# One unit's keys through DRAM, the last projection by rows, and a new order for an attention and feed-forward kernel

## The chip, the cores and the metric

The kernel runs on one core of a Trainium2 chip. The core has a matmul engine (TensorE, called PE in the profile; its weight loads are shown as PEld), a vector engine (DVE), a scalar engine (ACT), GpSimd (POOL, hardly used here) and SyncE (SP), whose queue issues all the transfers between on-chip memory (SBUF) and DRAM. Matmuls write to PSUM, eight banks of 128 x 512 f32. The engines run side by side and wait for each other by semaphores. The metric is device time in microseconds (us), the median of several executions; smaller is better.

## What is computed

The inputs are x (8 batches of 112 rows of 512) and a context (8 batches of 375 rows of 256). First comes cross attention with 16 heads of 128, then a feed-forward layer whose matmuls work on values rounded to 8-bit integers:

```
def attention(h, ctx):
    q = rmsnorm((h @ Wq).reshape(B, Sq, H, D), gq)
    k = rmsnorm((ctx @ Wk).reshape(B, Skv, H, D), gk)
    v = (ctx @ Wv).reshape(B, Skv, H, D)
    attn = softmax(einsum('bqhd,bkhd->bhqk', q, k) / sqrt(D))
    return einsum('bhqk,bkhd->bqhd', attn, v).reshape(B, Sq, H * D) @ Wo

def ffn(x):                                   # Q = 127
    a, sa = quantize_rowwise(x)               # round(x * Q / max|row|), max|row|
    w1, s1 = quantize_global(W1)
    h = gelu((a @ w1.T) * (sa * s1 / Q**2) + B1)
    b, sb = quantize_rowwise(h)
    w2, s2 = quantize_global(W2)
    return (b @ w2.T) * (sb * s2 / Q**2) + B2

x = x + attention(layernorm(x), ctx)
x = x + ffn(layernorm(x))
```

Inside the feed-forward layer, a row's layer norm multiplies the whole row by one positive number, the reciprocal root of its variance. Rounding by the row's largest magnitude divides that number out again, so the rounded row needs only x minus its mean; the root is wanted later, in the factor that scales the product back.

## The kernel before

The batches are taken in four pairs, and the 16 heads in four groups of four. A pair with a group is numbered G (16 of them, `NGG`), one batch with one group is a unit u (32). For each unit the kernel makes keys (three tiles of 128 context rows, 512 wide), norms and transposes them, makes scores against the transposed queries, a softmax, and weighs the context rows with the probabilities (`weigh`). Per G it then multiplies by the value weights (`values`) and by the output weights (`project`), whose result is added up, transposed, in the tile aT of the pair. After a pair's fourth group the sum is turned back to rows, added to x (`residual` or `sum_add`), and the feed-forward layer begins. The 112 rows of batch 0 are dealt out to the 16 spare rows of the other seven batches, so there are seven feed-forward batches. In the last pair, batches 6 and 7 are the tail: their hidden values are handled in four pieces of 512 columns to keep all engines going.

Nearly every transpose goes through DRAM: DVE transposes blocks of 32 x 32, four sends write the blocks to DRAM in their new places, and one fetch reads the whole back. Early work that cannot wait for this is transposed on PE by a matmul with the identity: the tokens of the first pair (`token_turn`), the first queries (`query_turn`), the first unit's keys (`key_turn`), the context rows of the first two batches (`rows_turn`) and the last unit's probabilities (`prob_turn`).

The order of all work is written out. Each step has a short name, and four scripts (one for each pair, given to `play`) list name.index words; the index counts from the script's pair, so that R.-6 in the fourth script is index 0. Within PE, DVE, ACT and SP the instructions run exactly in this order (`in_written_order`). An instruction that waits holds up all behind it on its engine, and a transfer that waits holds up all later transfers on SP. PSUM has two rings of four banks, one for scores and one for everything else (`mm_tile`); a new tile waits until the tile four before it on its ring has been read out. The names that matter here:

- kh, k0 to k2: key matmuls; kc copies them out of PSUM (ACT), kq squares (ACT), kr sums (DVE); ka, kb, ke, kd make the reciprocal root by Ln and Exp on ACT and a refinement on DVE; kn scales (DVE); kt makes blocks (DVE); ks sends, kf fetches (SP). kv and kw are the way through PE.
- xs, xa to xd, xm, xt, xk, xy: statistics, root, norm, turning and keeping of the tokens; index 7 is the last batch, whose rows are dealt out to the spare rows of the other batches' tokens.
- ct, ck: context rows through PE and their copies; cb, cs, cf, co: by blocks, send, fetch, ordering copy (ACT).
- Q, S, qt, qs, qf, G: queries, their sums of squares (ACT), blocks (DVE), send, fetch, gain; qv, qw, qx: the way through PE.
- s0 to s3 scores, x0 and x1 their maxima (DVE), e the exponentials (ACT), iv the reciprocal, n the scaling (ACT), z blocks (DVE), ps and pf send and fetch, pt and pk the way through PE; w weighing (PE) and v its copy (ACT).
- o, u, p, a: values, their copy, projection, addition for a whole pair; O, U, P, A the same for one batch, used for the last group alone.
- ra turns the sum back (PE), rb adds it to x (DVE); st statistics, fa to fd root, fi norm and maximum, fq rounding, ti and tj the turn of the rounded rows, h hidden matmuls, i their scaling and bias, g gelu (ACT), mx maxima, es scale, qp and qq rounding, tp and tk the turn, Y or y the output matmuls, yo the last addition, yd the send.
- jl, jm, ja, js, jr: loading the feed-forward weights in 1 MB pieces, their maxima (2.28 us each on DVE), scaling and rounding; lq, lk, lv, lo, lx, ly, lc, lf, l7: loads.

Before the first keys, PE runs `WARM` matmuls on zeros (L116).

Of the kernel before, what the change touches and what calls it, by code (L numbers as in the profile page):

```python
# [9 lines left out]
F32 = mybir.dt.float32  # L10
# [20 lines left out]
def xattn_ffn_kernel(  # L31
# [16 lines left out]
    nc = tc.nc  # L48
# [21 lines left out]
    WARM = 3  # L70
# [397 lines left out]
    def rows_turn(b, j0, j1):  # L468
        pt = T["pc", b] = mm_tile(f"pc_{b}_{j0}")
        for j in range(j0, j1):  # L470
            for k in range(KCC):
                nc.tensor.transpose(
                    pt[:, (j - j0) * CC + k * P : (j - j0) * CC + (k + 1) * P],
                    T["cT", b][:, k, j * P : (j + 1) * P], ident,
                )

    def rows_keep(b, j0, j1):
        if j0 == 0:
            T["c", b] = work.tile([P, NJ, CC], F32, tag="c", name=f"c_{b}", bufs=3)
        nc.scalar.copy(  # L480
            T["c", b][:, j0:j1, :].rearrange("p j c -> p (j c)"), T.pop(("pc", b))[:, : (j1 - j0) * CC]
        )

# [33 lines left out]
    for n, (j0, j1) in enumerate(((0, 2), (2, 3))):  # L517
        step(f"ct{n}", BP, rows_turn, j0, j1)
        step(f"ck{n}", BP, rows_keep, j0, j1)
        step(f"cb{n}", BP, rows_blocks, n)  # L520
        step(f"co{n}", BP, rows_order, n)
# [331 lines left out]
    def weigh(u, k):  # L853
        b = batch_of(u)
        after(*[((f"co{n}" if b >= BP else f"ck{n}"), b) for n in range(2)])
# [46 lines left out]
    def project(G, lo, n, c0):  # L902
        if n == TP:
            after(("u0", G), ("u1", G))
        else:
            after((f"U{lo // S}", G))
# [20 lines left out]

    for n in range(2):
# [6 lines left out]
        step(f"P{n}", NG, project, n * S, S, 0)  # L935
        step(f"A{n}", NG, project_add, n * S, S, 0)
# [19 lines left out]
    def turn_sum(b):  # L956

        p, i = divmod(b, BP)
        if p == NPAIR - 1:
            after((f"A{i}", NGG - 1))  # L960
        else:
            after(("a0", p * NG + NG - 1), ("a1", p * NG + NG - 1))
        pa = T["pa", b] = mm_tile(f"pa_{b}")
        for c in range(KC):
            nc.tensor.transpose(pa[:S, c * P : (c + 1) * P], T["aT", p][:, c, i * S : (i + 1) * S], ident)
# [47 lines left out]
    def stats(b):  # L1013
        after(("rb" if b >= B - BP else "rn", b), ("zf", b))
# [4 lines left out]
    def row_absmax(src, name):  # L1019
        m = small.tile([P, 1], F32, tag="rowmax", name=name)  # L1020
# [8 lines left out]
    def norm_in(b):  # L1029
        after(("fd", b))  # L1030
        xn = T["xn2", b] = ffn.tile([P, C], F32, tag="y", name=f"xn2_{b}")
        nc.vector.tensor_scalar(xn, x2_of(b), T["mv2", b][:, 0:1], T["rstd2", b], ALU.subtract, ALU.mult)
        T["m1", b] = row_absmax(xn, f"m1_{b}")
        T["d1", b] = dequant_scale(T["m1", b], absw1, f"d1_{b}")
# [6 lines left out]
    def quantize_in(b):  # L1041
        quantize_rows(home("xq", b, [P, C], BF16), T["xn2", b], quant_scale(T["m1", b], P))
# [41 lines left out]
    def hidden_keep(b, n):  # L1084
        after(("lb", 0))
# [27 lines left out]
    def pieces_scale(b):  # L1113
        after(*[(f"mx{n}", b) for n in range(NF4)])
        m = small.tile([P, 1], F32, tag="rowmax", name=f"m2_{b}")
# [71 lines left out]
    step("fi", BP, norm_in)  # L1187
    step("fq", BP, quantize_in)
# [18 lines left out]
    for n in range(2):  # L1207
# [7 lines left out]
        cz.0 lk.0 cz.1 lf.0 lf.1 lx.0 l7.0 gl.0 lc.1 kh.0 jl.0 lk.1 lq.0 jl.3 jl.6 kh.1 xs.1 xs.0 xa.1  # L1215
        xc.1 xs.7 ct0.0 kc0.0 xa.0 xb.7 k0.1 kc1.0 xb.1 xd.1 xc.0 xm.1 xa.7 kq0.0 xc.7 k1.1 kr0.0 kq1.0
        kc2.0 xb.0 xd.0 kc0.1 kr1.0 ck0.0 ct0.1 xm.0 kq2.0 xt.1 xd.7 kc1.1 cz.2 xt.0 kr2.0 ck0.1 k2.1
        kb.0 ka.0 xm.7 ke.0 kq0.1 kd.0 xk.0 kn2.0 xt.7 xk.1 gm.0 kn0.0 kv2.0 xk.7 jm.0 kc2.1 xl.0 kv0.0
        kq1.1 lq.1 k0.2 kw0.0 kw2.0 kn1.0 xy.0 xy.1 kr0.1 kv1.0 kr1.1 kq2.1 Q0.0 kr2.1 kb.1 ka.1 jm.3
        kc0.2 ke.1 Q1.0 qt0.0 kw1.0 qs0.0 lx.1 kd.1 jl.1 kn1.1 qv0.0 kn0.1 S0.0 kt0.1 k1.2 kq0.2 kn2.1  # L1220
# [181 lines left out]
```

## Time and profile before

| | |
|---|---|
| median of 3 runs | 719.77 us (719.55 to 721.48) |
| profiled execution | 720.28 us |
| its span | 718.5 us, so 1.78 us lie around it |
| PE busy | 702.7 us, 98% |
| DVE busy | 537.3 us, 75% |
| ACT busy | 433.6 us, 60% |
| DMA engines, mean busy share | 85% for the one queue in use |
| last matmul ends | 714.3 us |

The profile comes from one execution. Times in it count from the start of its span. "Idle before" is the time that an engine stood just ahead of an instruction, with the engine, tile and line that let it go on. A 512-column matmul of f32 is two passes in the trace, and passes overlap: the mean duration of one (593 ns for the keys) is longer than the time from one start to the next (0.43 us), which is what a pass costs when PE is full. A PE that is shown busy therefore means that passes lie close, and costs on PE are best taken from start to start.

### The profile page before, as it was taken

Reading aid. Unit: us, or ns where it says so; the run is one execution under the profiler, and the core shown is the slowest. Engines: PE = TensorE matmul, PEld = TensorE weight load, DVE = VectorE, ACT = ScalarE, POOL = GpSimd, SP = SyncE. Lnnn points to the kernel's source line nnn. Section 1 sums busy time; section 2 is a strip of 40 time slices with the busy share of each in tenths; the row PEclk is TensorE's granted clock in tenths of the full one; section 3 lists DMA queues with packets and bytes.
Section 4 is the critical chain, followed back from the end, with each engine's and each line's share of the span. In section 5 each row is a group of like instructions: output and inputs, shape, how many; then the busy total and the mean of one; then the engine's idle time right before and its main releaser. Section 6 shows DMA issues by size and latency. Waiting matters only on the chain.

```text
span 718.5 us, 8555 instructions
## 1 busy us (share of the span) xinstructions
PE 702.7 (98%) x2398; PEld 413.3 (58%) x2410; DVE 537.3 (75%) x1234; ACT 433.6 (60%) x1129; POOL 2.4 (0%) x10
## 2 busy tenths in 40 slices
PE   9999999999999999999999999999999999999976
PEld 4444456655657564745656465564657455667742
DVE  6997888887876677747857787868774898964395
ACT  5677576636475756556466556666755566627325
POOL 0000000000000000000000000000000000000000
PEclk9999999999999999999999999999999999999999
DMA  8799999989988999999898989999999889998201
GB/s 304 266 280 298 294 298 282 301 268 290 282 308 244 293 285 313 269 275 310 227 289 286 295 265 287 287 240 305 292 257 291 237 256 272 259 290 282 34 1 44
DMA packets 131246, 187.85 MB, mean 261 GB/s; under 512 B 34864, under 2 KB 90800, under 8 KB 130560
## 3 DMA queue, kind: packets, MB, share of 16 engines
q1 hardware_dynamic: 131200, 187.32, 85.1%
q8 instruction: 19, 0.31, 0.2%
q14 instruction: 27, 0.22, 0.1%
HBM read 124.55 MB, written 59.45 MB: 256 GB/s over the span
## 4 chain that ended last, share of the span: by engine, by line
PE 85%; DVE 5%; ACT 4%; DMA 3%; SPq 1%; issue 1%; POOL 0%; ACTq 0%; DVEq 0%; POOLq 0%
PE pkk L650 19%; PE pu L860 17%; PE pw L910 13%; PE pq L532 12%; PE sc L758 10%; PE po L887 6%; PE py L1159 2%; PE ph L1080 2%; DMA pT<-pd 1%; PE pkk L660 1%; DMA kT<-kd 1%; ACT probs L780 1%; DMA qr<-q 1%; DMA qss<-s 1%; ACT qsq L547 1%
## 5 line engine op out<-in xcount | busy, mean ns | idle before, releaser
L650 PE MATMUL pkk<-wk,cT 128*128 128x512 f32 x372 | 171.8, 593 | 0.3 <-DVE hid L1089 0.3
L860 PE MATMUL pu<-pT,c 128*128 128x448 f32 (+1 forms) x384 | 152.3, 540 | 1.0 <-DMA pT<-pd 1.0
L860 PEld LDWEIGHTS pu<-pT,c 128*128 128x128 f32 (+1 forms) x384 | 72.5, 190 | 71.3 <-issue 61.7
L780 ACT ACTIVATE probs<-sc,bias,rq 112x375 f32<-112x375 f32 x128 | 84.1, 663 | 47.8 <-DVE bias L773 47.8
L650 PEld LDWEIGHTS pkk<-wk,cT 128*128 128x128 f32 x372 | 70.0, 190 | 72.3 <-issue 60.9
L910 PEld LDWEIGHTS pw<-oT,wo 128*128 128x128 f32 x544 | 98.2, 190 | 9.8 <-issue 6.5
L910 PE MATMUL pw<-oT,wo 128*128 128x224 f32 (+1 forms) x544 | 101.8, 343 | 0.6 <-ACT oT L897 0.6
L532 PE MATMUL pq<-wq,xnT 128*128 128x512 f32 x224 | 100.2, 592 | 0.0
L758 PE MATMUL sc<-kT,qT 128*112 128x384 f32 x256 | 92.4, 486 | 0.3 <-DMA kT<-kd 0.2
L670 ACT COPY kk<-pkk 128x512 f32<-128x512 f32 x96 | 55.2, 580 | 58.6 <-DVE kz L698 25.6
L797 DVE STREAM_TRANSPOSE pz<-probs 128x384 f32<-128x384 f32 x120 | 63.7, 558 | 21.1 <-ACT probs L791 18.2
L791 ACT ACTIVATE probs<-probs,inv 112x375 f32<-112x375 f32 x128 | 72.1, 605 | 8.9 <-DVE inv L788 8.9
L771 DVE TENSOR_REDUCE top<-sc 112x1 f32<-112x375 f32 x128 | 63.8, 535 | 18.0 <-PE sc L758 17.5
L681 DVE TENSOR_REDUCE kss<-ksq 128x4 f32<-128x512 f32 x96 | 63.1, 668 | 14.0 <-ACT ksq L675 14.0
L532 PEld LDWEIGHTS pq<-wq,xnT 128*128 128x128 f32 x224 | 42.4, 190 | 49.6 <-issue 46.5
L758 PEld LDWEIGHTS sc<-kT,qT 128*112 128x112 f32 x256 | 44.7, 177 | 38.9 <-issue 16.7
L675 ACT ACTIVATE ksq<-kk 128x512 f32<-128x512 f32 x96 | 59.5, 628 | 6.4 <-DVE kss L681 6.0
L688 DVE TENSOR_TENSOR kk<-kk,rk 128x512 f32<-128x512 f32 x96 | 62.9, 675 | 0.5
L698 DVE STREAM_TRANSPOSE kz<-kk 128x512 f32<-128x512 f32 x93 | 62.3, 690 | 0.9 <-issue 0.4
L871 ACT COPY wc<-pu 128x448 f32<-128x448 f32 x64 | 33.5, 531 | 36.6 <-PE pu L860 36.6
L887 PEld LDWEIGHTS po<-wc,wv 128*128 128x128 f32 x272 | 49.1, 190 | 8.0 <-issue 4.1
L887 PE MATMUL po<-wc,wv 128*128 128x224 f32 (+1 forms) x272 | 53.1, 344 | 0.0
(122 smaller groups left out, 590.8 us busy)
## 6 DMA issues: line engine op xcount, KB each, us to landing
kd<-kz SPq DMA_DIRECT2D x124, 192.0 KB, 4.0
kT<-kd SPq DMA_DIRECT2D x31, 768.0 KB, 6.4
pT<-pd SPq DMA_DIRECT2D x30, 672.0 KB, 6.1
pd<-pz SPq DMA_DIRECT2D x90, 192.0 KB, 4.4
wq<-in_wq SPq DMA_DIRECT2D x16, 1024.0 KB, 7.7
wo<-in_wo SPq DMA_DIRECT2D x16, 1024.0 KB, 7.8
wv<-in_wv SPq DMA_DIRECT2D x16, 512.0 KB, 5.8
wk<-in_wk SPq DMA_DIRECT2D x15, 512.0 KB, 6.2
```

The lines of the kernel that those rows point to most:

```text
L532: nc.tensor.matmul(pq[:, :GW], T["xnT", p][:, k, i * P : (i + 1) * P], T["wq", G][:, k, :], start=(k == 0), stop=(k == KC - 1),)
L650: nc.tensor.matmul(pk[:, :GW], T["cT", batch_of(u)][:, k, j * P : (j + 1) * P], T["wk", u // BP][:, k, :], start=(k == 0), stop=(k == KCC ...
L681: nc.vector.tensor_reduce(T["kss", u][:, j, :], T.pop(("ksq", u, j)).rearrange("p (h d) -> p h d", d=D), AX.X, ALU.add)
L688: nc.vector.tensor_tensor(kv, kv, T["rk", u][:, j, :].unsqueeze(2).to_broadcast([P, HG, D]), ALU.mult)
L758: nc.tensor.matmul(sc[:S, :SKP].rearrange("p (j i r) -> p j i r", j=NJ, r=BK), T["qT", G, i][:, h, :], T["kT", u][:, :, :, h, :].rearrange ...
L771: nc.vector.tensor_reduce(top[:, h : h + 1], T["sc", u, h0 + h][:S, :SK], AX.X, ALU.max, negate=True)
L780: nc.scalar.activation(p_bufs[h][:S, :SK], T["sc", u, h][:S, :SK], AF.Exp, bias=T["bias", u, h0][:, h - h0 : h - h0 + 1], scale=rq_of(u, h ...
L791: nc.scalar.mul(p_bufs[h][:S, :SK], p_bufs[h][:S, :SK], T["inv", u][:, h : h + 1])
L797: nc.vector.transpose(T["pz", u][:, :, :, :, h, :].rearrange("p a f j q -> p j a f q"), p_bufs[h].rearrange("p (j a r) -> p j a r", j=NJ, ...
L860: nc.tensor.matmul(pu[:, : HG * S], T["c", b][: ROWS[j], j, k * P : (k + 1) * P], T["pT", u][: ROWS[j], :, j, :, :].rearrange("p f h q -> ...
L887: nc.tensor.matmul(po[:, (h - h0) * n : (h - h0 + 1) * n], T["wv", G][:, k, h * D : (h + 1) * D], T["wc", G][:, k, h, :, :].rearrange("p b ...
L910: nc.tensor.matmul(pw[:, (c - c0) * n : (c - c0 + 1) * n], T["wo", G][:, h, c * P : (c + 1) * P], T["oT", G][:, h, lo : lo + n], start=(h ...
```

## The change

1. `WARM` goes from 3 to 2.
2. `rows_turn` and `rows_keep` are gone: the context rows of batches 0 and 1 go by blocks and DRAM like those of the other six (cb, cs, cf, co).
3. The keys of unit 0 go by blocks and DRAM (kt, ks, kf); kv and kw are no longer called.
4. The last group's projection is made per batch with the transposed values as the stationary operand and the output weights as the moving one (`project_rows`, R). Its result stands in rows and is added to x directly (`rows_add`, rc). The sum of the first three groups is turned back and added before that (ra, rb).
5. The feed-forward norm (fi) only subtracts the mean, and no longer waits for the root; the root is multiplied into the row maximum in a new step (fe), which the hidden values' scaling (i) waits for.
6. All four scripts are ordered anew.

```
-    WARM = 3
+    WARM = 2
...
-    for n, (j0, j1) in enumerate(((0, 2), (2, 3))):
-        step(f"ct{n}", BP, rows_turn, j0, j1)
-        step(f"ck{n}", BP, rows_keep, j0, j1)
+    for n in range(2):
         step(f"cb{n}", BP, rows_blocks, n)
...
+    def project_rows(i):
+
+        after((f"U{i}", NGG - 1))
+        pr = T["pr", i] = mm_tile(f"pr_{i}")
+        for h in range(HG):
+            nc.tensor.matmul(
+                pr[:S, :], T["oT", NGG - 1][:, h, i * S : (i + 1) * S], T["wo", NGG - 1][:, h, :],
+                start=(h == 0), stop=(h == HG - 1),
+            )
+
+    def rows_add(i):
+        x2 = T["x2", NPAIR - 1][:S, i, :]
+        after(("rb", B - BP + i))
+        nc.vector.tensor_tensor(x2, x2, T.pop(("pr", i))[:S, :], ALU.add)
+
+    step("R", BP, project_rows)
+    step("rc", BP, rows_add)
...
-        step(f"P{n}", NG, project, n * S, S, 0)
-        step(f"A{n}", NG, project_add, n * S, S, 0)
...
     def turn_sum(b):
...
-        if p == NPAIR - 1:
-            after((f"A{i}", NGG - 1))
-        else:
-            after(("a0", p * NG + NG - 1), ("a1", p * NG + NG - 1))
+        after(("a0", NGG - 2), ("a1", NGG - 2))
...
     def norm_in(b):
-        after(("fd", b))
+
+
+        after(("st", b))
         xn = T["xn2", b] = ffn.tile([P, C], F32, tag="y", name=f"xn2_{b}")
-        nc.vector.tensor_scalar(xn, x2_of(b), T["mv2", b][:, 0:1], T["rstd2", b], ALU.subtract, ALU.mult)
+        nc.vector.tensor_scalar(xn, x2_of(b), T["mv2", b][:, 0:1], None, ALU.subtract)
         T["m1", b] = row_absmax(xn, f"m1_{b}")
-        T["d1", b] = dequant_scale(T["m1", b], absw1, f"d1_{b}")
+
+    def scale_in(b):
+        after(("fi", b), ("fd", b))
+        m = small.tile([P, 1], F32, tag="rowmax2", name=f"m1r_{b}")
+        nc.vector.tensor_tensor(m, T["m1", b], T["rstd2", b], ALU.mult)
+        T["d1", b] = dequant_scale(m, absw1, f"d1_{b}")
...
     def hidden_keep(b, n):
-        after(("lb", 0))
+        after(("lb", 0), ("fe", b))
```

The start of the first script and the end of the last, before and after:

```
-        cz.0 lk.0 cz.1 lf.0 lf.1 lx.0 l7.0 gl.0 lc.1 kh.0 jl.0 lk.1 lq.0 jl.3 jl.6 kh.1 xs.1 xs.0 xa.1
-        xc.1 xs.7 ct0.0 kc0.0 xa.0 xb.7 k0.1 kc1.0 xb.1 xd.1 xc.0 xm.1 xa.7 kq0.0 xc.7 k1.1 kr0.0 kq1.0
-        kc2.0 xb.0 xd.0 kc0.1 kr1.0 ck0.0 ct0.1 xm.0 kq2.0 xt.1 xd.7 kc1.1 cz.2 xt.0 kr2.0 ck0.1 k2.1
...
+        cz.0 lk.0 l7.0 cz.1 cz.2 lf.0 lf.1 lx.0 lc.1 xs.7 lv.0 gl.0 xb.7 kh.0 cb0.0 lk.1 lq.0 jl.0 jl.3
+        kh.1 xs.1 xs.0 xa.1 xa.7 xc.1 xb.0 xa.0 xb.1 xc.0 k0.1 xc.7 xd.0 kc0.0 xd.7 kq0.0 xm.7 kc1.0
+        kr0.0 k1.1 kc2.0 xd.1 kq2.0 xm.0 kq1.0 xm.1 kc0.1 kr1.0 xt.1 kc1.1 xt.7 kr2.0 xt.0 kb.0 ka.0
+        cb1.0 ke.0 k0.2 xk.7 kd.0 xk.0 xl.0 kn2.0 kq0.1 cs.0 kn1.0 xk.1 xy.1 kn0.0 k2.1 xy.0 kq1.1 kt0.0
+        kt2.0 Q0.0 kc2.1 kt1.0 kr0.1 ks.0 kr1.1 kq2.1 gm.0 kr2.1 kb.1 lx.1 k1.2 jm.3 qv0.0 kc0.2 ka.1
+        qw0.0 ke.1 cf.0 kd.1 Q1.0 qx0.0 qt0.0 kc1.2 kn2.1 qs0.0 S0.0 kn0.1 kf.0 kt0.1 lq.1 kn1.1 kt1.1
+        k0.3 S1.0 kt2.1 sa.0 qv1.0 sb.0 ks.1 xs.3 k1.3 kc0.3 xb.3 jm.0 kc1.3 kq0.3 s1.0 co0.0 qt1.0 k2.3
...
-        v0.6 qh0.-1 pt2.7 v1.6 pt1.7 qh1.-1 pk2.7 O0.3 pk1.7 te.-1 w0.7 U0.3 P0.3 v0.7 w1.7 A0.3 ra.0
-        v1.7 O1.3 rb.0 st.0 fb.0 U1.3 fa.0 P1.3 fc.0 fd.0 fi.0 fq.0 A1.3 ti.0 bo.0 ra.1 tj.0 rb.1 h0.0
-        st.1 h1.0 i0.0 fa.1 fc.1 h2.0 i1.0 g0.0 fb.1 h3.0 i2.0 fd.1 g2.0 fi.1 fq.1 i3.0 ti.1 y0.-1 tj.1
...
+        pt2.7 v0.6 w1.6 te.-1 ra.1 v1.6 pk2.7 O0.3 rb.1 n1.7 pt1.7 U0.3 ra.0 pk1.7 R.-6 rb.0 w0.7 rc.-6
+        st.0 fi.0 w1.7 v0.7 fq.0 fa.0 fc.0 ti.0 v1.7 tj.0 fb.0 h0.0 fd.0 fe.0 h1.0 i0.0 bo.0 g0.0 h2.0
+        i1.0 O1.3 i2.0 mx0.0 g2.0 h3.0 mx2.0 U1.3 g1.0 R.-5 i3.0 mx1.0 g3.0 mx3.0 es.0 qp1.0 qp0.0 y0.-1
+        rc.-5 qq0.0 st.1 fi.1 fa.1 y1.-1 fq.1 fc.1 qp2.0 ti.1 tj.1 qp3.0 h0.1 yo.-1 qq3.0 tp0.0 qq2.0
...
```

The sets of steps are otherwise the same, but some move from one script to the next: in the first script four of the weight pieces (jl.0, .3, .2, .1) instead of six are loaded before unit 0's context is weighed (w0.0), one of the second matrix's pieces (jl.4) is loaded only in the second script, and so is the load ly.0.

## The prediction

> **What bounds the kernel now.** First the page's list of engines, then the matmul engine's waits, then busy time by stretch, then the timeline's two ends.
>
> ```profile
> PE 702.7 (98%) x2398; PEld 413.3 (58%) x2410; DVE 537.3 (75%) x1234; ACT 433.6 (60%) x1129; POOL 2.4 (0%) x10
> ```
>
> TensorE (PE) is busy for 98% of the span, so only two things can shorten it: less PE work, or less of the 15.8 us in which PE stands. Where it stands (us in total, times, longest):
>
> ```profile
> PE pxq L1052 <- DVE xq L1039: 3.2, 1, 3.2
> PE phq L1052 <- ACT hq L1137: 1.6, 3, 0.8
> PE warm L116 <- POOL probs L111: 1.2, 1, 1.2
> PE pu L860 <- DMA pT<-pd: 1.0, 1, 1.0
> PE py L1159 <- ACT hqT L1060: 0.9, 1, 0.9
> ...
> PE pkt L725 <- DVE kk L688: 0.5, 1, 0.5
> ```
>
> Nearly all of it is at the end (L1052 and L1159 belong to the last feed-forward batches, and PE's last matmul ends at 714.3 of 718.5). The middle is dense. By stretch of 18 us (PE, weight loads, DVE, ACT, ...):
>
> ```profile
> 18.00:36.00 18.00, 17.55 (x62) 8.90 (x61) 17.13 (x31) 12.17 (x38) 0.00 (x0) 1.00 0.79 266
> 36.00:54.00 18.00, 17.36 (x56) 8.48 (x55) 16.16 (x35) 13.71 (x39) 0.00 (x0) 1.00 0.97 279
> 54.00:72.00 18.00, 18.00 (x48) 8.56 (x47) 14.19 (x40) 13.53 (x41) 0.00 (x0) 1.00 0.93 299
> ```
>
> From 18 to 54 us VectorE (DVE) is busy 33.3 of 36 us, almost as full as PE. The parts that the change takes away are these groups (busy us, mean ns, idle before):
>
> ```profile
> L910 PE MATMUL pw<-oT,wo 128*128 128x112 f32 x64 | 7.5, 276 | 0.6 <-ACT oT L897 0.6
> L116 PE MATMUL warm<-probs 128*128 128x384 f32 x6 | 4.2, 874 | 1.2 <-POOL probs L111 1.2
> L472 PE MATMUL pc<-ident,cT 128*128 128x128 f32 x12 | 2.0, 272 | 0.0
> L725 PE MATMUL pkt<-ident,kk 128*128 128x128 f32 x12 | 1.8, 277 | 0.5 <-DVE kk L688 0.5
> ```
>
> **The change, part by part.** The sum is made against the profiled execution: 720.28 us, its span of 718.5 and 1.78 around it. It lies 0.51 above the median of 719.77.
>
> *Context rows of batches 0 and 1 by blocks.* Twelve PE transposes go. Four of them start at 11.32 and the next matmul starts at 11.76, so they pace at 0.11 us: 1.3 us of PE (the row's 2.0 is the upper end). ACT's four copies (L480, 1.9 us) give way to four of 0.50. DVE gains four block transposes of 0.55; the first falls into the idle time before x lands (3.73 us). Eight sends and two fetches are added.
>
> *Unit 0's keys by DRAM.* Twelve PE transposes (start to next start, 1.01 for eight and 0.47 for four) and the 0.5 wait go: 2.0 us. DVE gains three block transposes of 0.69 and loses a copy of 0.65; ACT loses 1.1. Four sends and a fetch of 768 KB are added.
>
> These two free PE of 3.3 us before about 55 us. But DVE gains 3 x 0.69 + 3 x 0.55 - 0.65 = 3.1 us in the stretch where it has 2.7 us idle, and three weight maxima of 2.28 us stay there. So I follow the new order by hand, with these rows:
>
> - The last batch's rows (224 KB) now go first on SP's queue. At the 290 GB/s or so that the queues move in the first microseconds, that puts every later load back by 0.45 (an issue) to 0.8 us, x from 8.17 to about 8.9. The first key copy (L670) now waits on ACT behind three roots: about 11.4 instead of 9.80.
> - Key matmul k2.1 takes the PSUM buffer of batch 1's turned tokens, which ACT empties (xk.1) only after two key copies, a root, two token copies and a squaring: about 19.4, with PE there at 18.4. Wait 1.0; behind it on PE stand the first queries. The queries then start at 21.1 (22.33 before, 2.3 us of work fewer done).
> - Unit 0's keys are normalized and turned by about 22.1 (norms 0.68 x 3, blocks 0.69 x 3 after the root, 17.5 before, 18.0 now). The sends land 3.0 to 3.6 later, at 27.4. But the fetch stands on SP behind the query send, which waits for DVE's qt0.0, itself behind three sums, a 2.28 us maximum and a root: 28.1. Fetch issued 28.4. Landing: 4.1 us (448 KB at 27.30) to 8.6 (768 KB at 37.71); I take 5.7, the 1 MB load at 19.66, which like this one had a quiet queue. It lands at 34.1, while PE reaches s1.0 at 21.1 + 12.5 = 33.6. Wait 0.5 (0 to 3.4). Behind the fetch on SP stand the next query weights and unit 1's key sends, both wanted over 10 us later; behind s1.0 on PE, everything.
> - Unit 0's scaled probabilities come through x0.0, four exponentials (0.65 each), two key operations and n1.0: about 44.8, some 0.9 after PE. The next turn needs the query buffer that ACT empties after n3.0: 0.3.
>
> New waits 2.7 against 3.3 removed, and I add 0.3 for the 0.6 of issue wait at 47.91, which has no like place: head gain 0.9 us. The ends: 3.3 (no wait) and -2 (fetch 8.6 us).
>
> *One warm-up matmul fewer.*
>
> ```profile
> 5.19 6.29 PE L660 MATMUL pkk<-wk,cT 128*128 128x512 f32 x12
> ...
> 6.04 0.34 PEld L660 LDWEIGHTS pkk<-wk,cT 128*128 128x128 f32 x1 [0.52 <-issue]
> ...
> 6.90 0.32 PEld L660 LDWEIGHTS pkk<-wk,cT 128*128 128x128 f32 x1 [0.52 <-issue]
> ...
> 7.46 0.19 PEld L660 LDWEIGHTS pkk<-wk,cT 128*128 128x128 f32 x1 [0.24 <-issue]
> 7.89 0.19 PEld L660 LDWEIGHTS pkk<-wk,cT 128*128 128x128 f32 x1 [0.24 <-issue]
> ```
>
> The pace falls from 0.86 to 0.43 us between 6.90 and 7.46. Two warm-ups (1.28 each) end at about 3.8, and the context's first half, landed by 4.57 now, comes at about 5.2: a gap of 1.4 us, and the keys start when they did. I take 0. Ends: +0.2, and, if the slow pace lasted for all 12 passes, 12 x 0.86 - 6.1 = 4.2 lost. [...]
>
> *Last projection by rows.* Of each batch's 32 passes (3.72 and 3.83 us) 8 of 512 columns remain; eight such take 3.43 (L532): 0.7 us of PE less. More matters on the chain: addition A (0.62) and the turn back (0.6, standing behind 2.4 us of weighing for batch 6) leave it.
>
> *Roots beside quantization.* From the row statistics (681.35) to the normalization (683.30) 2.0 us leave the chain, for each batch; one product (0.2) is added, beside matmuls.
>
> *The tail in the new order*, in the profile's times: R.0 672.5 to 675.9; residual, statistics, subtraction and maximum, quantization (0.69, 0.9, 1.25, 1.3) end at 680.4; ti.0 at 680.6 (686.11 before). But the values of batch 7 now stand behind three hidden matmuls, 684.5 to 686.5 (679.5 before), R.1 ends at 690.9, its addition waits on DVE behind es and two qp until 691.3, and ti.1 is at 695.6 against 694.65. After it less lies between: h3.1 ends at 700.9 (701.7). Batch 7's Ln now follows gelu, so two more table loads of 1.28, the second ahead of g0.1. The last maximum ends at 704.7 (706.46); from there 7.7 as before: gain 2.1 us (ends 0.5 and 3.8).
>
> *The middle.* Same PE work in another order. It had 1.7 us idle between 468 and 612; I take no change (ends +1.5, -2). Of the 3.1 MB of added DMA traffic, 10 us at 290 GB/s where the queues are 0.79 to 0.97 busy, the cover is two 1 MB weight pieces and x rows issued later than before; without it the fetches would be late by as much.
>
> **Sum.** 718.5 - 0.9 - 2.1 = 715.5, with 1.78 around it 717.3; less 0.5 for the median: 716.8.
>
> **Rivals.** (1) *PE stays dense in the head.* For: before, only 1.1 us idle from 18 to 54. Against: DVE at 92%. 3.3 + 0.5 (a warm-up's worth and the middle) + 2.2: 713.8. (2) *The head's saving is eaten, by DVE or by a longer slow pace (up to 4.2).* For: DVE's 36.4 us of work in 36, and the gap of 1.4 us before the keys. The tail alone stays, and up to its 2.1 is lost: 717.7 to 721.5, middle 719.5. (3) *Slower: unit 0's fetch is late.* Everything from s1.0 hangs on it, and SP serves qs0.0 first. If DVE reaches qt0.0 2 us later and the fetch takes 8.6, s1.0 waits 5.3, 4.8 above my case: 721.6. From 5.6 us of wait on the kernel is slower than before by 0.3%; with 6: 722.3. Against: the queue is quiet there. (4) *The tail doesn't do what it says*, as batch 7 was moved back: 718.9.
>
> **How the numbers follow.** My case 0.38 (715.3 to 717.9), rival 1 0.25 (712.5 to 715), rival 2 0.14, rival 3 0.13, rival 4 0.10. A measurement tells 0.3%, 2.2 us, from no change. Faster (below 717.6): 0.25 + 0.33 = 0.58; slower (above 721.9): rival 3's 0.10 and 0.03 of rival 2: 0.13; within: 0.29. The range leaves out a quarter of rival 1 and most of rival 3, together less than 2 in 10: 713.0 to 721.8.
>
> **What would show it.** Right: no L472 and L725 groups; PE waits before 55 us of 2 to 3 us, on ACT xnT, DMA kT and ACT probs; DVE over 95% from 18 to 54; the stretch from the first hidden matmul of batch 6 starting 5 us earlier before the end than now; ACT_TABLE_LOAD twice more; the wait of pxq on xq below 2 us. Wrong: passes of 0.86 us beyond 8 us; a PE wait on kT above 3; a PE idle time of over 3 us in the middle; or PE as dense as before in the head.

## The result and the profile after

The changed kernel takes 728.57 us (median of 6 runs, 724.51 to 733.53) against 719.66 us for the kernel before beside it (median of 6, 719.09 to 722.67): ratio 1.0116, 95% interval 1.0079 to 1.0153. It is 8.9 us slower, and the forecast of 716.8 us (713.0 to 721.8) missed it by 12. The profiled execution of the changed kernel is one of its slower ones, 733.53 us with a span of 730.6, so the places below add up to 12.1 us (730.6 - 718.5) and not to 8.9.

From the page of the changed kernel: engines; the transfers' queue (packets, MB, share of its 16 engines' span); the chain that ended last, by engine.

```profile
PE 703.9 (96%) x2336; PEld 405.8 (56%) x2336; DVE 543.6 (74%) x1247; ACT 436.7 (60%) x1130; POOL 2.4 (0%) x10
...
q1 hardware_dynamic: 133360, 190.47, 85.9%
...
PE 56%; DMA 24%; DVE 7%; SPq 5%; ACT 5%; issue 1%; DVEq 0%; ACTq 0%
```

The same two lines of the kernel before that were not shown yet:

```profile
q1 hardware_dynamic: 131200, 187.32, 85.1%
...
PE 85%; DVE 5%; ACT 4%; DMA 3%; SPq 1%; issue 1%; POOL 0%; ACTq 0%; DVEq 0%; POOLq 0%
```

PE has almost the same work (703.9 us against 702.7). But 24% of the chain that ended last now are transfers, 3% before. PE stands waiting for them (us in total, times, longest), changed kernel:

```profile
PE pu L842 <- DMA pT<-pd: 10.6, 7, 3.2
PE pkk L642 <- DMA cT<-in_ctxT: 2.3, 1, 2.3
PE sc L740 <- DMA kT<-kd: 1.8, 3, 1.2
PE sc L740 <- ACT qT L608: 1.6, 1, 1.6
...
PE ph L1079 <- DVE xqT L1059: 1.0, 2, 0.5
PE pxq L1051 <- DVE xq L1037: 1.0, 1, 1.0
```

The first line was 1.0 us in one wait before: PE is ready to weigh the context rows, and the probabilities (pT) have not come back from DRAM. The old longest wait, `pxq` on `xq` (3.2 us in the tail), is down to 1.0. By stretch (PE, weight loads, DVE, ACT, GpSimd busy, granted clock, DMA share, GB/s), changed kernel:

```profile
18.00:36.00 18.00, 18.00 (x51) 8.43 (x50) 17.42 (x33) 12.73 (x42) 0.00 (x0) 1.00 0.91 290
36.00:54.00 18.00, 17.94 (x58) 8.98 (x58) 17.36 (x43) 14.52 (x47) 0.00 (x0) 1.00 0.99 315
108.00:126.00 18.00, 16.25 (x50) 8.93 (x49) 13.38 (x31) 12.50 (x27) 0.00 (x0) 1.00 0.92 281
...
324.00:468.00 144.00, 140.84 (x443) 80.62 (x442) 100.06 (x233) 81.56 (x237) 0.00 (x0) 0.99 0.90 273
```

and one of the kernel before:

```profile
324.00:468.00 144.00, 143.90 (x466) 83.61 (x467) 109.85 (x251) 88.05 (x232) 0.00 (x0) 1.00 0.90 279
```

The head is dense (18.00 and 17.94 of 18 us) and the tail is shorter; the middle, idle for 0.1 us in this stretch before, is idle for 3.2 us in it. Three marks in PE's timelines of the two profiled executions say where the time went. The first values of group 0 start at 90.50 us, at 93.08 before; one key projection of 1.72 us still has to be done, so the lead is 0.9 us. The second weighing of unit 30 starts at 683.18, at 666.27 before: 16.9 us later. From there to the end it takes 47.4 us, 52.2 before. Head -0.9, middle +17.8, tail -4.8: together 12.1.

The largest single loss lies at 405.7 us (PE's timeline of the changed kernel: start, length, line, operation, count, idle before):

```profile
403.78 1.88 PE L632 MATMUL pkk<-wk,cT 128*128 128x512 f32 x4
408.82 6.45 PE L842 MATMUL pu<-pT,c 128*128 128x448 f32 x12 [3.15 <-DMA pT<-pd]
```

and, right behind it, the same kernel's busy times with the granted clock in the column after GpSimd:

```profile
410.10:413.50 3.40, 3.40 (x6) 1.51 (x5) 0.00 (x0) 0.53 (x1) 0.00 (x0) 0.50 1.03 303
```

PE waits 3.15 us for the probabilities of unit 16, and then its clock is halved for 3.413 us (the trace's clock record, 410.1 to 413.5). The twelve passes take 6.45 us; the same twelve take 4.68 at full clock, at 692.20. So this costs 1.8 us more.

To see why, each unit's way was followed in both traces: from the end of its last block transpose on DVE to the start of its weighing on PE. "Slack" is what lies between the landing of the fetch and the weighing; "send and fetch" are the two times from issue to landing, added.

| units 1 to 30 | before | changed |
|---|---|---|
| send and fetch, median | 12.3 us | 11.9 us |
| last block to weighing, median | 17.1 us | 18.0 us |
| slack, median | 2.96 us | 2.15 us |
| units with a slack of 0.5 us or less | 3 | 10 |

The round trip through DRAM has not become slower in the median. It takes 12 us in both kernels, with outliers to 16.7 us before and 17.7 now, and the new order leaves more units with nothing to spare. Before, nearly every fetch landed within its slack, and no view of waits showed how near that was.

The medians of the rows do not add up, and one of them misleads: in the mean, the order leaves 17.1 us now from the last block to the weighing, 18.7 before. The seven waits are of two kinds. For units 9, 26 and 29 (waits of 1.43, 1.43 and 2.00 us) the new order is short: 11.5 to 12.7 us, where the old one had 14.6 to 23.8. For units 4, 16 and 25 (1.21, 3.15 and 1.23 us) it leaves some 20 us, but their sends start up to 5.2 us late on SP's queue or take up to 11.9 us (5.9 in the median). The seventh is 0.19 us.

### The profile page after: what moved, and what is told of

It is laid out like the page before. It is cut to its first block, busy times and chain, and to the rows that moved or that the text cites. A ratio compares the mean times of both kernels' runs of the same rounds, so it can differ in the third digit from the quotient of the medians.

```text
span 730.6 us, 8472 instructions
## 1 busy us (share of the span) xinstructions
PE 703.9 (96%) x2336; PEld 405.8 (56%) x2336; DVE 543.6 (74%) x1247; ACT 436.7 (60%) x1130; POOL 2.4 (0%) x10
## 4 chain that ended last, share of the span: by engine, by line
PE 56%; DMA 24%; DVE 7%; SPq 5%; ACT 5%; issue 1%; DVEq 0%; ACTq 0%
PE pu L842 13%; PE pkk L632 12%; PE pq L514 8%; PE sc L740 6%; DMA pT<-pd 6%; PE pw L889 6%; PE po L869 4%; DMA wq<-in_wq 3%; DMA kd<-kz 3%; DMA wo<-in_wo 3%; PE ph L1079 2%; SPq L689 2%; PE py L1158 2%; DMA kT<-kd 2%; DMA qr<-qd 2%; DMA pd<-pz 2%
## 5 line engine op out<-in xcount | busy, mean ns | idle before, releaser
L842 PE MATMUL pu<-pT,c 128*128 128x448 f32 (+1 forms) x384 | 154.2, 545 | 10.6 <-DMA pT<-pd 10.6
L740 PE MATMUL sc<-kT,qT 128*112 128x384 f32 x256 | 94.1, 488 | 3.4 <-DMA kT<-kd 1.8
L889 PEld LDWEIGHTS pw<-oT,wo 128*128 128x128 f32 x480 | 90.8, 190 | 7.2 <-issue 3.6
L889 PE MATMUL pw<-oT,wo 128*128 128x224 f32 x480 | 94.2, 352 | 0.0
L680 DVE STREAM_TRANSPOSE kz<-kk 128x512 f32<-128x512 f32 x96 | 64.5, 692 | 11.2 <-DMA kd<-kz 10.4
```

The lines of the kernel that those rows point to most:

```text
L680: nc.vector.transpose(T["kz", u][:, :, j, :, :].rearrange("p a h r -> p h a r"), T["kk", u][:, j, :].rearrange("p (h a r) -> p h a r", h=H ...
L740: nc.tensor.matmul(sc[:S, :SKP].rearrange("p (j i r) -> p j i r", j=NJ, r=BK), T["qT", G, i][:, h, :], T["kT", u][:, :, :, h, :].rearrange ...
L842: nc.tensor.matmul(pu[:, : HG * S], T["c", b][: ROWS[j], j, k * P : (k + 1) * P], T["pT", u][: ROWS[j], :, j, :, :].rearrange("p f h q -> ...
L889: nc.tensor.matmul(pw[:, (c - c0) * n : (c - c0 + 1) * n], T["wo", G][:, h, c * P : (c + 1) * P], T["oT", G][:, h, lo : lo + n], start=(h ...
```

## The experiments

The order is a list of words, so kernels can be mixed: the words of one up to a join, then those of the other that are left, in its order. Head means up to the keeping of group 0's second values, tail from the first weighing of unit 30 on. Indices of words count through the whole kernel here. Each run is compared with the kernel before, run beside it on the same chip (medians 721.46 to 722.05 us); differences in us are differences of these medians, and the ratio comes with its interval.

### Head, middle and tail apart

Tail alone:

```
-    (before, to the end)
+    (before, up to w0.30) (changed, the words that are left)
```

> Head and middle in the order of the kernel before; only what comes from the first weighing of unit 30 on is the changed kernel's (last projection by rows, its roots beside the quantization, its order). Theory 1, the order of the middle loses the time and the tail by itself gains: in the two traces the stretch from the weighing of unit 30 to the end is 51.9 us before and 47.2 us after, so 719.7 - 4.6 = 715.1 us (713.5 to 717). Theory 2, the tail of the changed kernel only looks shorter because its middle is late and so its side work (DVE, ACT, DMA) was already done: my own price of the tail, 2.1 us, or less: 717.5 to 719.7 us.

Middle back:

```
-    (changed, to the end)
+    (changed, up to u1.0) (before, up to w0.30) (changed, the words that are left)
```

> The changed kernel's head (keys of unit 0 and context rows by DRAM, two warm-up multiplications, its order up to the keeping of the first values) and its tail, with the steps between them in the order of the kernel before. Theory 1, the order of the middle: the head gives 0.9 us and the tail 4.6 us, so 719.7 - 5.5 = 714.2 us (712.5 to 716.5). Rival, the 3.1 MB more of DMA and the late start of the head are behind the later waits: 726 to 729 us, as the changed kernel.

Head alone:

```
-    (before, to the end)
+    (changed, up to u1.0) (before, the words that are left)
```

> Only the head of the changed kernel, everything after the first values in the order of the kernel before. Theory 1: 719.7 - 0.9 = 718.8 us (717.5 to 720). Rival, the head's DMA and its late start push everything behind them: 728 to 734 us, since the tail's gain is then missing too.

Middle alone:

```
-    (before, to the end)
+    (before, up to u1.0) (changed, up to w0.30) (before, the words that are left)
```

> Only the middle in the changed kernel's order (from the first values to the weighing of unit 30, with the roots of these batches beside their quantization); head and tail are the kernel before's. Theory 1: the changed kernel is 8.9 us slower although its head and tail gain 5.5 us, so this order costs 14.4 us: 734 us (730 to 738). Rival, the head is the cause: 719 to 721 us.

| | median, us | before, us | ratio, 95% interval |
|---|---|---|---|
| tail alone | 720.11 | 722.05 | 0.9981 (0.9962 to 0.9999) |
| middle back | 727.37 | 722.05 | 1.0067 (1.0040 to 1.0095) |
| head alone | 729.21 | 722.05 | 1.0107 (1.0085 to 1.0128) |
| middle alone | 734.80 | 722.05 | 1.0188 (1.0157 to 1.0219) |

My theory, that the middle's order loses all and head and tail gain, is half right. The middle alone loses 12.8 us, about what it said. But the tail alone gains 1.9 us and not 4.6, and the head alone does not gain 0.9: it loses 7.2, and with the old middle between the new head and tail the kernel is 5.3 us slower than before, as the rival had it. The trace of the head alone shows where: up to the first values it is ahead as in the changed kernel, and then, from 116.7 us on, the old middle waits for it (PE's waits, head alone):

```profile
PE sc L758 <- DMA kT<-kd: 4.2, 2, 2.9
...
PE pkk L650 <- DVE aT L923: 1.4, 1, 1.4
```

So there was something besides the order: in 108 to 126 us of this run the DMA engines were at a share of 1.01 (a packet is counted whole in the stretch in which it starts). The rival, that transfers are what is short, had to be tried.

### Transfers added, and transfers left out

Six steps of transfers that nobody reads, added to the kernel before in the head. They are 3.1 MB in 19 transfers; the changed head has the same bytes in 15.

```
+    def spare_send(b, keys):
...
+                nc.sync.dma_start(
+                    out=t[a : a + m, :, i, :].rearrange("a r n -> r a n"),
+                    in_=rows.rearrange("r (a n) -> r a n", n=n),
+                )
+    def spare_fetch(b, keys):
...
+        nc.sync.dma_start(out=to, in_=t.rearrange("a r i n -> (a r) (i n)"))
-    kn2.0 ... Q0.0 ... ke.1 ... S0.0 ... e3.0 ... w0.0
+    kn2.0 Ds0.0 ... Q0.0 Ds1.0 ... ke.1 Df0.0 ... S0.0 Df1.0 ... e3.0 Ds0.1 ... w0.0 Df0.1
```

> The kernel before with six more transfers that nobody reads: the same 3.1 MB, at about the same places as the changed head's (context rows of two batches and unit 0's keys, out to DRAM and back, there from DRAM to DRAM). Theory C, the transfers of the first 60 us (DMA share 0.86 to 0.97 there) are at their limit and 3.1 MB at some 300 GB/s push all later ones back by up to 10 us: 4 to 9 us slower than before. Rival, there is room for them and the head's loss is the order of its instructions: within 1.5 us of before.

Measured 728.56 us, 6.8 us slower than before (ratio 1.0077, 1.0053 to 1.0101). Transfers alone, with no instruction of PE, DVE or ACT changed, do it. The waits are new (kernel before with added transfers):

```profile
PE pu L860 <- DVE x L392: 2.4, 1, 2.4
PE sc L758 <- DMA kT<-kd: 2.2, 4, 0.7
...
PE pkk L650 <- DMA wk<-in_wk: 1.1, 1, 1.1
```

The view puts the first of them down to DVE, but the fetch of the probabilities that this weighing uses landed at 84.64, 0.13 us ahead of its start, so PE waits again for a fetch of the probabilities. A halved clock of 3.413 us follows it (the mean granted clock of this execution is 0.993, 0.999 in that of the kernel before).

The same six later, in the middle of the kernel before:

```
-    k1.19 ... k2.19 ... w1.15 ... o0.7 ... k1.20 ... k0.21
+    k1.19 Ds0.4 ... k2.19 Ds1.4 ... w1.15 Df0.4 ... o0.7 Df1.4 ... k1.20 Ds0.5 ... k0.21 Df0.5
```

> The kernel before with the same 3.1 MB of transfers that nobody reads, now issued between 358 and 391 us instead of the first 60 us. Theory C, transfers have no room anywhere: 3 to 7 us slower than before, as in the head. Rival, the slack of 3 us (median) that this order leaves behind each fetch of the probabilities takes it up, and only the head is short: within 1.5 us of before.

Measured 729.64 us, 8.1 us slower (ratio 1.0108, 1.0081 to 1.0135). The slack does not take them up. PE's waits for keys, of which the one of 3.9 us lies at 373 us, among the added transfers:

```profile
PE sc L758 <- DMA kT<-kd: 6.0, 2, 3.9
```

How that wait came about can be read from SP's timeline, of this kernel and then of the kernel before:

```profile
366.84 4.54 SPq L1253 DMA_DIRECT2D sp<-cT  x8
371.43 0.43 SPq L714 DMA_DIRECT2D kT<-kd  x1
```

```profile
365.20 0.40 SPq L714 DMA_DIRECT2D kT<-kd  x1
```

The fetch of the keys stands behind the added sends and is issued 6.2 us later than before, although its own sends landed at 364.0 (364.1 before). Once issued it takes 5.6 us, 5.2 before. So here the added transfers cost their places in the one queue, and hardly any slower landing. The two runs with added transfers do not tell the price of bytes from the price of places in the queue.

Now the other way. A quarter of each weight piece, in the changed kernel and in the head alone:

```
-            in_=srcT[i * n_k * P : (i + 1) * n_k * P, :].rearrange("(k p) n -> p k n", p=P),
+        nc.sync.dma_start(out=st[:, :part], in_=srcT[i * n_k * P : (i * n_k + 1) * P, :part])
+        nc.gpsimd.memset(st[:, part:], 0.01)
```

> The changed kernel, but of each of the eight 1 MB pieces of the hidden layers' weights only a quarter is loaded and the rest is filled on GpSimd with a constant, so the output is not the reference's: 6.3 MB fewer in the first 150 us. Theory C: the waits of the first 180 us go (0.4, 1.6, 1.2 and 0.6 us) and perhaps 1.5 us of the late start; 722 to 725 us. Rival, transfers are not what holds it: 727 to 730 us.

> The changed head with middle and tail in the order of the kernel before (7.2 us slower than before by the last runs), with the same quarter of the weight pieces loaded, so the output is not the reference's. Theory C: waits of 1.4 and 2.9 us and the half clock behind them at 116 to 124 us go, 718.5 to 722 us. Rival, VectorE and ScalarE, which have more to do in this head, are what is late there: 727 to 730 us.

723.37 us (ratio 1.0009, 0.9984 to 1.0034) and 723.91 us (1.0015, 0.9991 to 1.0039): the changed kernel is 1.6 us slower than before instead of 8.9 (1.1 without one of its ten runs, of 731.94), the head alone 2.1 instead of 7.2, which lies between the two ranges that were named for it. Then 12% fewer bytes, spread over the whole span (167.9 MB instead of 191.0 in the changed kernel):

```
     def load_wq(G):
...
+        half = KC // 2
+        nc.sync.dma_start(
+            out=t[:, :half, :], in_=wq[: half * P, bass.ts(G % NG, GW)].rearrange("(k p) n -> p k n", p=P)
+        )
+        nc.gpsimd.memset(t[:, half:, :], 0.01)
```

> The changed kernel with a tenth fewer bytes: of each weight load of the queries and of the output projection only half, of each piece of the hidden layers' weights only a quarter, the rest filled on GpSimd with a constant, so the output is not the reference's (22 MB fewer of 191, spread over the span). Theory C, the middle loses because its round trips run through transfers that have no room left, not because its instructions stand in a worse order: the change then is worth what I had counted, 2 to 3 us faster than the kernel before with the same loads left out: 716 to 719 us. Rival, the order by itself is too tight whatever the transfers do: most of the 7 us of waits left with quarter pieces stay, 722 to 726 us.

> The kernel before with the same loads left out (the output is not the reference's); the partner of the run of the changed kernel with fewer bytes. Its trace has 1 us of waits in the middle and 2 us in the head, so both theories expect 718 to 721 us.

> Head and tail of the kernel before, the middle in the changed kernel's order (13.7 us slower than before by the run of this mixture), with the same loads left out (the output is not the reference's). Theory C: within 3 us of the kernel before with fewer bytes, 718 to 723 us. Rival, the order itself: 726 to 734 us.

| with fewer bytes | median, us | ratio to before with all bytes | with all bytes |
|---|---|---|---|
| changed kernel | 718.14 | 0.9953 (0.9937 to 0.9969) | 1.0116 |
| kernel before | 721.42 | 1.0004 (0.9985 to 1.0023) | 1 |
| middle alone | 727.68 | 1.0092 (1.0058 to 1.0126) | 1.0188 |

This is the run that decides. With 12% fewer bytes in the same number of transfers (720) the same change, in the same order, makes the kernel 3.3 us faster (718.14 against 721.42). I had counted 0.9 + 2.1 = 3.0, but that this is so near is chance: the middle alone still loses here, and the tail turns out below to be worth more than 2.1. The kernel before gains nothing from fewer bytes. The output projection's weights (load_wo) are halved in the same way. PE's waits in the changed kernel with fewer bytes:

```profile
PE pu L867 <- DMA pT<-pd: 2.6, 1, 2.6
PE pkk L667 <- DMA cT<-in_ctxT: 2.0, 1, 2.0
PE sc L765 <- ACT qT L633: 1.7, 1, 1.7
```

Of seven waits for pT one is left, at unit 29. Send and fetch are down to 10.9 us in the median, and the slack is 3.46 us, with two units at 0.5 or less. The middle alone shows that this is not all: at 727.68 us it lies where the rival had it, and still loses 6.3 us with fewer bytes, half of what it loses with all. So the order is tighter by itself, and the bytes that were left out double what that costs.

### Is it the head's bytes, or one place?

The changed order without the added bytes:

```
-    cb0.0 ... cb1.0 ... cs.0 ... kt0.0 kt2.0 ... kt1.0 ... ks.0 ... cf.0 ... kf.0 ... co0.0 ... co1.0
+    ct0.0 ck0.0 ... kv0.0 kw0.0 kv2.0 kw2.0 ... kv1.0 kw1.0 ... ct1.0 ... ck1.0
                                            (and so for the context rows of batch 1)
```

> The changed kernel's order and tail, but unit 0's keys and the context rows of batches 0 and 1 are turned by TensorE as before, each step where its counterpart through DRAM stood: 3.1 MB fewer, 24 small transposes more (2.6 us of TensorE), which the kernel before has as well. If the added bytes are all that is wrong: before less the tail's gain, 719.5 to 721 us. If the parts add as measured (tail -1.6, head +6, the middle's order given its head +3.5): 723 to 724.5 us. If this middle needs the head it was made with: 728 us or more.

Measured 739.01 us (ratio 1.0234, 1.0194 to 1.0274), worse than the changed kernel. The first values of group 0 start 7.8 us later in it than in the changed kernel; 2.6 us of that is the work of the transposes, and the rest are waits at the places where I put them (0.9, 1.4 and 1.9 us the longest). So as a whole kernel it says little. Its middle says something: from the first values to the second weighing of unit 30 it takes 592.8 us; the changed kernel takes 592.7 and the kernel before 574.9, with the key projection of 1.72 us that stands ahead of the mark there. So, as far as one trace of each can tell, the loss of the middle is not an echo of the 3.1 MB in the head.

Six weighings later:

```
-    w0.4 ... w1.4 ... k2.9 ... Q0.4        (and so for units 9, 16, 25, 26, 29)
+    k2.9 w0.4 w1.4 ... Q0.4
```

> The changed kernel with the two weighings of units 4, 9, 16, 25, 26 and 29 moved one to three of TensorE's steps later (behind the third projection of unit 9, the first of unit 14, the first queries of group 10, the last scores of unit 27, the last projection of unit 31, the second scores of unit 31), nothing else. Theory A, these weighings stand too close behind their probabilities' way through DRAM: their waits in the changed kernel's trace (1.2, 1.4, 3.2, 1.2, 1.4, 2.0 us, 10.5 us together, and 1.7 us of half clock behind the longest) go, 718 to 723 us. Theory B, something else (transfers, VectorE or ScalarE) runs at its limit and TensorE only waits for it where it meets it: the waits come back at the next consumer, 726 to 730 us.

Measured 742.14 us (ratio 1.0263, 1.0210 to 1.0317). Both theories fail: it is 20.4 us slower than before, where the changed kernel is 8.9. What steps into the gap is no more ready than what was there. The scores that moved up wait for their keys' way through DRAM, longer than the weighings had (PE's longest group of waits in this kernel):

```profile
PE sc L758 <- DMA kT<-kd: 11.7, 4, 4.7
```

and the clock is halved in four places, twice for 6.8 us (mean granted clock 0.986). Here a wait was not cured by letting the next chain take its place.

The last hidden multiplication of batch 5 in front of unit 29's weighing:

```
-    x1.29 h3.5 x0.29 ... i3.5 ... ge.5 ... lm.5 ... w0.29
+    x1.29 x0.29 ... h3.5 w0.29 i3.5 ... s1.31 ge.5 ... e1.31 lm.5
```

> The changed kernel with the last hidden multiplication of batch 5 moved from before the values of group 13 to just ahead of the weighing of unit 29, where the kernel before has it, its three followers (hidden kept, gelu, largest) behind it. The wait of unit 29 (2.0 us; 2.6 us with fewer bytes, 3.5 us in the middle alone) is then covered by 1.7 us of work: 1.5 to 2.5 us faster than the changed kernel, 726 to 727 us. Rival, the chain behind the scores of group 13 then waits instead: no change, 728 to 729 us.

Measured 727.64 us in the median of four runs (725.65, 727.09, 728.20 and 737.70; ratio 1.0078, 1.0055 to 1.0100). It is 6.1 us slower than before, or 5.6 without the run of 737.70, the changed kernel 8.9, but the two intervals overlap, and unit 29 still waits 2.23 us in its trace. Inconclusive.

One load moved back behind the first tokens:

```
-    cz.0 lk.0 l7.0 cz.1 cz.2 lf.0 lf.1 lx.0
+    cz.0 lk.0 cz.1 cz.2 lf.0 lf.1 lx.0 l7.0
```

> The changed kernel with one load moved: the last batch's tokens (224 KB) behind the first pair's tokens, as before, and no longer second in the queue. Unit 0's halves should land 1 to 1.4 us sooner (3.3 and 4.5 us instead of 4.7 and 6.7 us after their issue, in the two traces). If what the start saves is kept: 1 to 2 us faster than the changed kernel's 728.6. If transfers set the pace of the first 160 us, the lead is waited off again: within 0.5 us of it.

The first keys start at 4.76 us instead of 6.45, but the kernel takes 730.57 us (ratio 1.0114, 1.0088 to 1.0140), as the changed one does (1.0116). PE meets its next inputs before they are there, waits 1.0 and 1.1 us on ACT, and starts the queries at 22.36 instead of 21.84. What starts sooner does not end sooner.

### The tail

Joined one unit later:

```
-    (before, to the end)
+    (before, up to w0.31) (changed, the words that are left)
```

> Head and middle of the kernel before up to the weighing of unit 31, the changed tail only from there (the earlier run of the tail joined it at the weighing of unit 30 and waited 1.9 us for the last probabilities). Without that wait: 3 to 3.5 us faster than before, 718 to 719 us. If the wait only moves to the next link of that chain: 1.5 us faster, as the earlier run.

Measured 716.21 us (715.39 to 717.71; ratio 0.9935, 0.9913 to 0.9957). This beats both kernels: 5.3 us by the medians, 4.7 by the ratio. The marks in the traces had been right about the tail; the first join had lost most of it, 1.9 us of it in one wait for the last probabilities, with a halved clock of 3.413 us behind it (mean granted clock 0.998 there, 1.000 here). PE's timeline of this kernel, the turns of the rounded rows of batches 6 and 7 (686.11 and 694.65 in the kernel before):

```profile
679.50 0.39 PE L1083 MATMUL pxq<-ident_h,xq 128*128 128x128 bf16 x4
...
685.64 3.61 PE L933 MATMUL pr<-wo,oT 128*112 128x512 f32 x8
689.08 3.62 PE L1190 MATMUL py<-wff,hqT 128*128 128x512 bf16 x15
693.67 0.40 PE L1083 MATMUL pxq<-ident_h,xq 128*128 128x128 bf16 x4 [0.97 <-DVE xq L1070]
```

Each of its two parts alone in the old tail:

```
-    U0.15 P0.15 v0.31 w1.31 A0.15 ra.6 ... U1.15 fa.6 P1.15 ... A1.15 ti.6 bo.6 ra.7
+    ra.7 ... U0.15 ra.6 R.0 ... w1.31 rc.0 ... U1.15 fa.6 R.1 ... rc.1 ti.6 bo.6
```

> The kernel before with the last projection by rows alone (the sum of the first three groups turned back and added ahead of it; the roots stay ahead of the normalization). By the forecast's terms: 0.7 us less of TensorE for each batch and 1.2 us (addition and turn back) off the chain of batch 6: 1.5 to 2.5 us faster than before. If it is this part that was sized too low: 3 to 4 us faster.

```
-    rb.6 st.6 fb.6 U1.15 fa.6 P1.15 fc.6 fd.6 fi.6 fq.6 A1.15 ti.6
+    rb.6 st.6 fi.6 fq.6 fb.6 U1.15 fa.6 P1.15 fc.6 A1.15 ti.6 fd.6 fe.6        (batch 7 likewise)
```

> The kernel before with only the roots of the last two batches beside their quantization (subtract the mean first, multiply the root in later), projection as before. By the forecast's terms: 2.0 us off the chain of batch 6, and little for batch 7, whose chain lies beside other work: 1.5 to 2 us faster than before. If this part was sized too low: 3 us faster. The two alone add up to the 5 us of the tail, or the order of the two together gives the rest.

721.12 us (ratio 0.9989, 0.9972 to 1.0006) and 721.29 us (1.0006, 0.9995 to 1.0016): neither gains anything measurable alone. (The 0.7 us of TensorE in my forecast was for both batches together, not for each.) With rows alone the long wait stays as it was (PE's timeline):

```profile
695.84 0.40 PE L1083 MATMUL pxq<-ident_h,xq 128*128 128x128 bf16 x4 [3.23 <-DVE xq L1070]
```

With roots alone it falls to 1.56 us and the waits behind it grow. The gain comes from the two in the order that goes with them: batch 6's rows are turned 6.6 us sooner, and the second projection by rows and the output of batch 5 then fill the time in which DVE prepares batch 7. The two parts together in the old order were not tried.

## Why the prediction was wrong

**The step that failed** is the middle's term, put at nothing: "Same PE work in another order. It had 1.7 us idle between 468 and 612; I take no change (ends +1.5, -2)." In the profiled execution it lost 17.8 us, and alone in the kernel before this order loses 12.8. The reason I gave, the same PE work, was true and did not bear on the time. What the order sets is how long each round trip has until PE wants it. The waits of the kernel before (1.0 us in all on pT) told that its 30 round trips were in time, not that the median one had 2.96 us to spare and needed 12.3. The runs show both halves: the order by itself is tighter (middle alone, 6.3 us with fewer bytes), and with all bytes it costs twice as much (12.8 us).

**"The cover is two 1 MB weight pieces and x rows issued later"** failed too, as a reason. Nothing covers them: 3.1 MB put into the kernel before cost 6.8 us in the head and 8.1 us in the middle, places in the queue included, and without 6.3 MB of the weight pieces the changed kernel is 1.6 us slower than before and not 8.9. The profile's mean is 261 GB/s in both kernels, and the head alone moves 346 GB/s from 108 to 126 us, which looks like a quarter to spare. But the transfers' share of the DMA engines is 85%, and the runs with added transfers lose time: the mean rate does not show room.

**The head's 0.9 us** came out as 0.9 up to the first values, by other terms than mine and so by luck; the same head leads there by 1.4 and 2.6 us in the traces of the head alone and of the middle back. The waits that I listed (1.0, 0.5, 0.3 and their like) did not come: PE is dense from 18 to 54 us although DVE is busy for 34.8 of these 36 (97%, "over 95%" was right), which was the sign of my first rival. The start lost what this gained. The first keys start at 6.45 us instead of 5.19 and take 7.52 us instead of 6.29 (changed kernel):

```profile
1.19 2.93 PE L116 MATMUL warm<-probs 128*128 128x384 f32 x4 [1.19 <-POOL probs L111]
6.45 7.52 PE L642 MATMUL pkk<-wk,cT 128*128 128x512 f32 x12 [2.33 <-DMA cT<-in_ctxT]
13.80 3.60 PE L632 MATMUL pkk<-wk,cT 128*128 128x512 f32 x8
```

I had the context's first half land at 5.2, with 0.45 to 0.8 us of delay by the load put ahead of it; it was issued at 1.64 and landed 4.67 later, at 6.3. (My 290 GB/s was too high there: between 2 and 9 us the kernel before moves 245.) "I take 0", with keys that start when they did, was therefore wrong by 2.0 us (13.80 against 11.76 for unit 1's first keys), within the end of 4.2: 1.3 for the later first key and 1.2 for slower passes, less 0.4 for four transposes that are gone. The weight loads of the first keys are 0.86 us apart up to 9.99, the sign I had named as wrong ("beyond 8 us"). That a gap ahead of the keys (2.33 us here) makes the slow pace last longer, as my second rival had it, was a guess: PE has no gap there in the kernel before. From the first key to the next matmul behind the twelve it is 7.35 us now and 6.13 before, 1.2 us more. In two other traces with the same two warm-ups (middle back, head undone) a gap of 2.0 us cost nothing: the twelve take 5.39 us there. So this price differs from one execution to the next.

**The tail's 2.1 us** was too small: 5.3 us by the medians, 4.7 by the ratio, above my outer end of 3.8. The mechanism was right as one order, and wrong as a sum of parts, 0.7 of PE, the addition and the turn back, 2.0 of roots: alone, neither part measured anything. The mis-sized term is batch 7's, "ti.1 is at 695.6 against 694.65". In the version with only the tail it is at 693.67, since the second projection by rows ended at 689.2 and not at 690.9, and from there to the end 19.8 us remain, 23.9 before. Of the marks I named: the wait of pxq below 2 us was right (1.0), three tables were loaded more and not two, and the first hidden matmul of batch 6 starts 2.3 us further from the end (33.0 against 30.7), not 5.

**The rivals.** None was the case. The third, which was to be slower, looked for one late fetch in the head. That one landed at 34.19 us (34.1 by my sum), and PE did not wait for it. The trouble was in round trips of the same kind, those of the probabilities, in the part that I had called unchanged: PE waited for seven of thirty. "A PE idle time of over 3 us in the middle" was my sign of a wrong prediction, and it came: 3.15 us at 405.7.

**What stays open.** How the 12.8 us of the middle alone divide between single places isn't settled: the weighings at six such places, moved in one run, only left their waits to others, and unit 29 waits 1.7 to 3.5 us in every kernel with this middle in which its weighing stayed in its place. Whether bytes or places in the one queue set the price of added transfers is open too. And the changed kernel's own head and its own middle lose less together (some 14 us, its 8.9 and the tail's gain of about 5) than apart (7.2 and 12.8); that each is fitted to the other's pace is likely, but no run shows it.

## What to carry to other kernels

Before an order is called "the same work", take each round trip by transfers and measure from its landing to its use, in the old trace, and count what stands between its issue and its use in the new order; a trace without waits tells nothing of that slack. Where the transfer engines are at 85% over the whole span, price added transfers by putting dummy ones into the old kernel, in the places where the real ones would stand in the queue; one run gives the number (here 6.8 and 8.1 us for 3.1 MB). Doubt every "covered". And parts of a chain should be tried with the order that goes with them: here two parts that gave nothing alone gave some 5 us together, and that version, without the rest of the change, is the one to keep.

## What was not expected of the hardware

In the trace of the changed kernel PE's granted clock is halved once, from 410.10 to 413.51 us, just behind the wait of 3.15 us that ended at 408.82. This piece of 3.413 us costs up to 1.8 (6.45 us instead of 4.68 for the twelve passes at 408.82 above), so that the wait comes to some 4.9 us. Behind the seven other waits of 1.2 to 2.0 us between 124 and 664 us in this trace the clock is full.

Not every long wait has a halved clock behind it. In the kernel before PE waits 3.24 us for the last rounded rows (up to 694.65), and in the middle back 3.27 us for keys (up to 122.09), and the granted clock stays at 1.00 behind both. In the head alone PE waits 2.94 us for the same keys (up to 122.92), and the mean granted clock is 0.94 from 108 to 126 us and 0.97 from 126 to 144. What sets these cases apart is left open. So a wait of some 3 us cost PE 3 us or some 5 here, and a kernel with many such waits shows it in its mean granted clock: 0.986 to 0.993 in the four executions with the six weighings moved, 0.999 to 1.000 in the four with the tail joined later, whose trace has no wait of PE above 1.2 us.
